# Another leaf order at the end of ff1's last outer product, and a searched order on the engines, in a fp32 transformer block on one core

## The chip, the core and the metric

The kernel runs on one core of one Trainium2 chip. A core has a matrix engine (TensorE, PE in the profile; PEld is its loading of weights), a vector engine (VectorE, DVE), an activation engine (ScalarE, ACT), a general engine (GpSimd, POOL) and a queue engine (SyncE, SP) that here issues nearly all transfers between the chip's main memory and the on-chip memory. Matrix results land in eight accumulation banks (bank0 to bank7), from which VectorE or ACT must read them ("evict" below) before the bank is used for something else.

The metric is the device time of one execution in microseconds (us), the median of several. All numbers below are us unless marked ns.

## The reference

Everything is fp32. `x` is 2 x 2048 x 512, `t` (the input `cond_1024`) 2 x 512, ssm weights 512 x 512, ff weights 512 x 1024 and 1024 x 512.

```python
emb = jnp.dot(jax.nn.silu(t), ada_w) + ada_b
shift_msa, scale_msa, gate_msa, shift_mlp, scale_mlp, gate_mlp = jnp.split(emb, 6, axis=-1)
norm = _ln(x) * (1.0 + scale_msa[:, None]) + shift_msa[:, None]
h = jax.nn.gelu(jnp.dot(norm, ssm_w1) + ssm_b1, approximate=False)
ssm_out = jnp.dot(h, ssm_w2) + ssm_b2
x = x + gate_msa[:, None] * ssm_out
norm2 = _ln(x) * (1.0 + scale_mlp[:, None]) + shift_mlp[:, None]
hf = jax.nn.gelu(jnp.dot(norm2, ff_w1) + ff_b1, approximate=True)
ff_out = jnp.dot(hf, ff_w2) + ff_b2
x = x + gate_mlp[:, None] * ff_out
```

## The kernel before

**Tiles and stages.** The 4096 rows are cut into eight blocks of 512. Per block there are the first normalisation (`norm1`), the two ssm products (`ssm1`, `ssm2`), the second normalisation (`norm2`); then, in four stages of two blocks each, the first feed-forward product (`ff1`) and, block by block, the second (`ff2`). Between these the weights are prepared: `weight2` scales the second ssm weight by the gate, `weight_fw1` and `weight_fw2` do the like for the feed-forward weights and write parts of them to main memory, from where `ff1` loads them again.

**Products of quarters.** Each matrix product is done by a fast scheme with seven products of quarter matrices instead of eight: `first` (L420) and `second` (L430) make the sums of quarters that go in, named P1 to P7 together with the quarters used as they are, and the seven products are added into each other's results. ff1 uses the scheme on two levels: seven outer products, in the order P1, P2, P6, P7, P4, P5, P3 (`OUTER`), each with seven inner ones, the leaves. A leaf is two 128x128x256 matmuls, and a matmul shows as two records in the trace. The inner order is `CARRIED` (L445): P1, P5, P6, P2, P7, P3, P4.

**Banks in a leaf order.** Of one outer product the leaves P1, P6, P7 and P4 add into one bank (called y), P2 into a second (x), which begins as a copy of P1 that ACT makes, and P5 and P3 into a third (v) (`BANK`). After each leaf but P1, VectorE adds the bank to the hidden quarters in `hidden` that this leaf belongs to. So P6 may only start when ACT has copied P1 away, P7 when P6 is evicted, P4 when P7 is evicted, P3 when P5 is. In `ff1` (function `leaf`, L1055) consecutive outer products overlap: the last three leaves of one alternate with the first three of the next. The last outer product has nothing behind it, so its last four leaves stand alone, one right behind the other; the outer product before it (P5) is evicted in pieces of 128x1024.

**Who sets the order.** Nothing is issued where the code calls it. Each helper (`tt` for adds of two tensors at L256, `act` L274, `copy` L283, `mm` L294, `turn_by_pe` L304, `dma` L316) records an operation with a cost in ns per engine it may run on ("v" VectorE, "g" POOL, "a" ACT, "p" TensorE, "s" SP). `tt` on data in on-chip memory may go to VectorE or to POOL. `Plan.order` gives each operation a latest start, from due times on TensorE, and `Plan.simulate` then runs through all operations by these costs and lays down engine and place of each; TensorE's operations keep the order of the code. The resulting order is a fixed program. Transfers are modelled as one pipe of 370 bytes per ns with a flight and a landing time, and eight lanes.

**The start.** L1366 copies a mask; then VectorE makes statistics of four row groups of the first block (`BATCH_NORM_STATS2` L522 and its aggregate L523), POOL and VectorE turn them into scales (L555, L556 on POOL, L558 to L561 on VectorE), VectorE (L581) and ACT (L274) normalise, PE turns the rows (L304), and after the modulation rows of `ada_w` the first ssm product begins. L1354 copies conditions and biases, transposed by PE after a row of warming matmuls, out of a bank into `cols`.

Of the kernel before, what the change touches and what calls it, by code (L numbers as in the profile page):

```python
# [1 line left out]

# [12 lines left out]


class Op:
    __slots__ = ("n", "engs", "fn", "cost", "lat", "shared", "size", "lead", "care", "after", "done", "sooner", "deps", "succ", "late", "on", "start", "end", "note")


class Plan:
# [5 lines left out]


    HOP = 70.0
    ISSUE, FLIGHT, LANDING, RATE, BACKLOG = 640.0, 1300.0, 700.0, 370.0, 4000.0  # L30
    NEAR, SPARE = 30000.0, 1500.0
    RATED, LANDED = 0.5, 4000.0
    LITTLE = 1 << 15
    LANES = 8
    AHEAD, SLACK = 2500.0, 150.0

    def __init__(self, nc):
        self.nc = nc
# [47 lines left out]
        return op  # L86

    def order(self):
        ops = self.ops
        for op in ops:  # L90
            if op.engs == "p":
                op.deps = {d for d in op.deps if ops[d].engs != "p"}
            for d in op.deps:
                ops[d].succ.append(op.n)
        t, due = 0.0, {}
        for op in ops:
            if op.engs == "p":
                due[op.n] = t
                t += op.cost["p"]
        for _ in range(2):  # L100
            for op in reversed(ops):
                late = due.get(op.n, 1e9)
                for s in op.succ:
                    late = min(late, ops[s].late - (1 + op.care) * (self.HOP + min(op.lat.values()) + op.size / self.RATE))
                op.late = late - op.sooner
            self.simulate()
            wait = ops[self.anchor].start - due[self.anchor]
            due = {n: t + wait for n, t in due.items()}
        return sorted(ops, key=lambda op: (op.start, op.n))

    def simulate(self):
        ops, hop = self.ops, self.HOP
        left, ready = [len(op.deps) for op in ops], [0.0] * len(ops)
        free = dict.fromkeys("pvags", 0.0)
        self.lock, pipe, holder = 0.0, 0.0, None
        tensor = [op for op in ops if op.engs == "p"]
        at, pools, found = 0, {e: [] for e in "vags"}, {}
        lanes = [0.0] * self.LANES

        def enter(op):  # L120
            if op.lead and op.late < 1e8:
                ready[op.n] = max(ready[op.n], op.late - op.lead)
            for e in op.engs:
                if e != "p":
                    pools[e].append(op)
                    found.pop(e, None)

        def choose(e):
            pool = pools[e]
            if not pool:  # L130
                return None
            at = {}
# [19 lines left out]
        count = len(ops)  # L152
        while count:
# [12 lines left out]
            if op.size > self.LITTLE:  # L166
                pipe = max(start + self.FLIGHT, pipe) + op.size / self.RATE * (1 + self.RATED * op.care)
                op.end = pipe + self.LANDING + self.LANDED * op.care
                found.pop("a", None), found.pop("s", None)
            else:  # L170
                op.end = start + op.lat[e]
                if op.size and e == "s":
                    op.end = max(op.end, pipe + self.LANDING)
            if op.size:
                lanes = lanes[1:] + [op.end]
                found.pop("a", None), found.pop("s", None)
            if e in op.shared:
# [10 lines left out]
            count -= 1  # L188
# [10 lines left out]
def kernel(  # L199
# [153 lines left out]
    for n in range(8):  # L353
        t = psum.tile([P, 2 * HT], F32, tag=f"bank{n}", name=f"bank{n}")
# [88 lines left out]
            tt(e, o[:, r], a[:, r], b[:, r], f)  # L443

    CARRIED = ("P1", "P5", "P6", "P2", "P7", "P3", "P4")  # L445

# [343 lines left out]

    def ssm1(i, ops, wops, hooks={}, order=CARRIED):
        plan.stage = f"ssm1 {i}"
# [97 lines left out]
    OUTER = ("P1", "P2", "P6", "P7", "P4", "P5", "P3")  # L892
# [131 lines left out]
    def ff1(s):  # L1024
        plan.stage = f"ff1 {s}"
        ops = tokens(s)
# [26 lines left out]
        QUAD = {"P2": "11", "P5": "22", "P6": "12", "P7": "22", "P3": "12", "P4": "21"}  # L1053

        def leaf(n, j):  # L1055
            p, f = OUTER[n], CARRIED[j]
            bank = {"y": Y_AT[n], "x": X_AT[n % 2], "v": V_AT[n % 2]}
            t = pair(bank[BANK[f]])
            src = cut(inner[n][f], "p a (c q) -> p c a q", q=G)
            half, at = divmod(FW1_AT[f], 4)  # L1060
            for h in range(2):
                mm(t[:, h, :], slot[n][half][:, at, h * P : (h + 1) * P], src, f in ("P1", "P5") and h == 0, f in ("P2", "P3", "P4"))
            if f == "P1":
                copy(pair(bank["x"]), t)
# [352 lines left out]
    for i in range(1, NBLK):  # L1417
# [4 lines left out]
        last = i + 2 >= NBLK  # L1422
# [76 lines left out]
```

## Time and profile before

| | |
|---|---|
| median of 3 executions | 566.46 (566.42 to 566.55) |
| profiled execution, own time | 566.59 |
| its span, first to last instruction | 564.8 |
| PE busy | 557.8, 99% |
| DVE busy | 483.1, 86% |
| POOL busy | 379.0, 67% |
| ACT busy | 266.0, 47% |
| granted TensorE clock | 1.000 |
| moved by transfers | 119.85 MB, mean 212 GB/s |

The profiled execution is 0.13 above the median, and 1.8 of it lie outside the span. A row of the timeline reads: start from the span's beginning, length, engine, line, operation, output tile, input tiles, shapes, and how many equal neighbours it joins; in brackets the idle time of the engine before it and what ended that. Matmuls are pipelined and their ends are modelled, so a row of PE is read by its start against the start of the next.

### The profile page before, as it was taken

What the parts mean: (1) busy time and instruction counts of PE and PEld (TensorE: products, weight loads), DVE (VectorE), ACT (ScalarE), POOL (GpSimd) and SP (SyncE); (2) the same over time, 40 slices, a digit from 0 to 9 for tenths busy, and PEclk for the clock granted to TensorE, in tenths of its full rate; (3) what the DMA queues carried; (4) which work ended last, traced back from release to release, by engine and by line L of the source; (5) the groups of instructions that cost most, each with busy time, mean ns of one, the idle gap of its engine ahead of it and who ended that gap; (6) DMA issues with size and microseconds to landing.
All of it is one profiled execution on the core that took longest, in us unless ns stands there. A gap on an engine that the chain in (4) does not pass through costs nothing.

```text
span 564.8 us, 10322 instructions
## 1 busy us (share of the span) xinstructions
PE 557.8 (99%) x3553; PEld 506.3 (90%) x3553; DVE 483.1 (86%) x918; ACT 266.0 (47%) x534; POOL 379.0 (67%) x514
## 2 busy tenths in 40 slices
PE   8999999999999999999999999999999999999997
PEld 4888889888898988889999889999889999888997
DVE  5696978888879989898989899999999888789776
ACT  3473856674888845557102347212366122336120
POOL 2887638979826687995547866776776784446660
PEclk9999999999999999999999999999999999999999
DMA  8953799989799879895047899078956041820022
GB/s 315 398 221 87 233 343 308 316 240 320 223 268 369 257 271 273 273 323 185 4 147 255 302 286 332 18 204 282 321 172 198 2 151 46 272 95 28 1 75 74
DMA packets 53057, 119.85 MB, mean 212 GB/s; under 512 B 5473, under 2 KB 10509, under 8 KB 51470
## 3 DMA queue, kind: packets, MB, share of 16 engines
q1 hardware_dynamic: 51842, 118.66, 63.9%
q8 instruction: 28, 0.46, 0.3%
q10 hardware_dynamic: 1164, 0.55, 0.3%
q14 instruction: 23, 0.19, 0.1%
HBM read 77.63 MB, written 40.51 MB: 209 GB/s over the span
## 4 chain that ended last, share of the span: by engine, by line
PE 94%; DVE 3%; DMA 1%; issue 1%; POOL 0%; SPq 0%; DVEq 0%
PE bank L294 94%; DMA fw<-in_L_cond_ada_w_dram 1%; DVE hidden L256 1%; DVE near L256 0%; DVE marks L522 0%; PE bank L304 0%; POOL hidden L256 0%; POOL near L256 0%; SPq L316 0%; DVE rows L256 0%; DVE ring L256 0%; DVE fw L256 0%; DVE far L591 0%; DVE turned L656 0%; DVE marks L523 0%
## 5 line engine op out<-in xcount | busy, mean ns | idle before, releaser
L294 PE MATMUL bank<-turned,ring 128*128 128x256 f32 x896 | 208.7, 380 | 0.2 <-DVE turned L656 0.2
L294 PEld LDWEIGHTS bank<-turned,ring 128*128 128x128 f32 x896 | 167.6, 190 | 22.9 <-DVE turned L656 0.5
L256 DVE TENSOR_TENSOR hidden<-bank,hidden 128x512 f32<-128x512 f32 (+1 forms) x171 | 125.2, 755 | 28.0 <-PE bank L294 24.8
L294 PE MATMUL bank<-near,hidden 128*128 128x256 f32 (+1 forms) x470 | 95.3, 350 | 0.3 <-DVE rows L256 0.2
L294 PEld LDWEIGHTS bank<-near,hidden 128*128 128x128 f32 x470 | 82.1, 190 | 10.0 <-DVE rows L256 0.6
L294 PE MATMUL bank<-fw,hidden 128*128 128x128 f32 x640 | 90.4, 275 | 0.0
L256 DVE TENSOR_TENSOR rows<-bank,rows 128x128 f32<-128x128 f32 (+3 forms) x154 | 78.8, 554 | 11.4 <-PE bank L294 10.9
L294 PE MATMUL bank<-ring 128*128 128x256 f32 x336 | 82.4, 381 | 0.5 <-DVE hidden L256 0.5
L294 PEld LDWEIGHTS bank<-fw,hidden 128*128 128x128 f32 x640 | 81.2, 192 | 0.4
L283 ACT COPY bank<-bank 128x512 f32<-128x512 f32 (+2 forms) x88 | 37.3, 425 | 83.3 <-PE bank L294 82.2
L256 POOL TENSOR_TENSOR turned<-turned 128x512 f32<-128x512 f32 (+1 forms) x56 | 63.1, 1139 | 16.7 <-ACT turned L274 9.4
L294 PEld LDWEIGHTS bank<-ring 128*128 128x128 f32 x336 | 63.2, 190 | 11.2 <-issue 1.7
L294 PE MATMUL bank<-fw,far 128*128 128x128 f32 (+2 forms) x644 | 67.6, 278 | 0.7 <-DMA fw<-in_L_cond_ada_w_dram 0.7
L294 PEld LDWEIGHTS bank<-fw,far 128*128 128x128 f32 (+1 forms) x644 | 60.9, 167 | 2.7 <-issue 1.7
L274 ACT ACTIVATE hidden<-hidden,cols 128x512 f32<-128x512 f32 (+1 forms) x66 | 45.0, 712 | 37.9 <-DVE hidden L256 37.8
L294 PE MATMUL bank<-fw,near 128*128 128x128 f32 (+1 forms) x452 | 61.1, 279 | 0.0
L256 POOL TENSOR_TENSOR hidden<-hidden 128x128 f32<-128x128 f32 (+2 forms) x52 | 43.6, 847 | 22.6 <-DVE hidden L256 6.4
L294 PEld LDWEIGHTS bank<-fw,near 128*128 128x128 f32 x452 | 56.0, 192 | 0.4
L256 POOL TENSOR_TENSOR fw<-fw 128x256 f32<-128x256 f32 (+1 forms) x52 | 45.0, 875 | 13.3 <-DVE fw L256 7.7
L274 ACT ACTIVATE turned<-turned,mod,mod 128x512 f32<-128x512 f32 x56 | 41.5, 805 | 8.2 <-DMA turned<-turned 7.2
L256 POOL TENSOR_TENSOR ring<-turned,ring 128x256 f32<-128x256 f32 x37 | 27.8, 757 | 15.8 <-PE bank L294 9.7
L256 DVE TENSOR_TENSOR hidden<-hidden 128x512 f32<-128x512 f32 (+2 forms) x58 | 34.9, 621 | 1.2 <-ACT hidden L274 0.8
(136 smaller groups left out, 692.4 us busy)
## 6 DMA issues: line engine op xcount, KB each, us to landing
ring<-fw_parts SPq DMA_DIRECT2D x28, 512.0 KB
turned<-far SPq DMA_DIRECT2D x52, 256.0 KB
ring<-fw_parts SPq DMA_DIRECT2D x28, 384.0 KB
rows<-x SPq DMA_DIRECT2D x32, 256.0 KB
turned<-turned SPq DMA_DIRECT2D x32, 256.0 KB
out_dram<-rows SPq DMA_DIRECT2D x28, 256.0 KB
fw_parts<-fw SPq DMA_DIRECT2D x21, 256.0 KB
fw<-in_L_cond_ada_w_dram SPq DMA_DIRECT2D x5, 1024.0 KB
```

The lines of the kernel that those rows point to most:

```text
L256: lambda E: E.tensor_tensor(o, a, b, f),
L274: lambda E: E.activation(o, a, func, bias=bias, scale=scale),
L283: plan.add("a", lambda E: E.copy(o, a), [o], [a], {"a": cost}, {"a": cost + 60})
L294: lambda E: E.matmul(o, lhsT, rhs, start=start, stop=stop, skip_group_check=True, **kw),
```

## The change

1. The leaves of ff1's last outer product take the order `ALONE`: P1, P6, P5, P7, P2, P3, P4. So P6 changes places with P5, and P7 with P2. The other outer products keep `CARRIED`.
2. The planner no longer makes one plan. It makes a first one, measures it in `follow` under four assumptions (`CASES`: landing time, transfer rate, length of the work on VectorE, ACT and POOL), notes the gaps on TensorE that are over 30 ns, and then 600 times asks some operations in front of a gap to come sooner (or their rivals later), draws up the plan again, and keeps it if TensorE ends earlier, at first also if it ends slightly later. The best is issued.
3. `WAKE`: the modelled transfer pipe delivers nothing before 2.2 us.

Only places and engines of operations differ: 109 adds go from POOL to VectorE and 85 from VectorE to POOL. TensorE has the same matmuls, in the same order but for 1.

```diff
+    WAKE = 2200.0
+    ROUNDS, WARMTH, LEAST = 600, 300.0, 30.0
+    CASES = ((700.0, 1.0, 1.0), (2200.0, 1.0, 1.0), (1200.0, 0.85, 1.0), (700.0, 1.0, 1.03))
...
+        self.draw_up({})
+        wait = ops[self.anchor].start - ops[self.anchor].due
+        for op in tensor:
+            op.due += wait
+        draw = random.Random(1)
+        wanted, (cost, gaps) = {}, self.draw_up({})
+        best = cost, wanted
+        for n in range(self.ROUNDS):
+            other = dict(wanted)
...
+                other[sooner] = other.get(sooner, 0.0) + more
+            found = self.draw_up(other)
+            if found[0] <= cost + draw.random() * self.WARMTH * (1 - n / self.ROUNDS):
+                wanted, (cost, gaps) = other, found
+                if cost < best[0]:
+                    best = cost, wanted
+        self.draw_up(best[1])
         return sorted(ops, key=lambda op: (op.start, op.n))
+
+    def draw_up(self, wanted):
+
+        ops = self.ops
+        for op in reversed(ops):
+            late = min([ops[s].late for s in op.succ], default=1e9) - op.ahead
+            op.late = (op.due if op.engs == "p" and op.due < late else late) - op.sooner - wanted.get(op.n, 0.0)
+        self.simulate()
+        last = dict.fromkeys("pvags")
+        for op in self.sequence:
+            op.before, last[op.on] = last[op.on], op.n
+        cost, gaps = 0.0, []
+        for case in self.CASES:
+            cost += self.follow(*case, gaps) / len(self.CASES)
+        return cost, gaps
...
-        self.lock, pipe, holder = 0.0, 0.0, None
+        self.lock, pipe, holder = 0.0, self.WAKE, None
...
     CARRIED = ("P1", "P5", "P6", "P2", "P7", "P3", "P4")
+    ALONE = ("P1", "P6", "P5", "P7", "P2", "P3", "P4")
...
         def leaf(n, j):
-            p, f = OUTER[n], CARRIED[j]
+            p, f = OUTER[n], (CARRIED, ALONE)[n == 6][j]
```

More of the change, by code (lines that the diff above doesn't have):

```diff
@@ L1 @@
+import random
 from contextlib import ExitStack
@@ L17 @@
 class Op:
-    __slots__ = ("n", "engs", "fn", "cost", "lat", "shared", "size", "lead", "care", "after", "done", "sooner", "deps", "succ", "late", "on", "start", "end", "note")
+    __slots__ = ("n", "engs", "fn", "cost", "lat", "shared", "size", "lead", "care", "after", "done", "sooner", "deps", "succ", "ahead", "before", "due", "late", "on", "start", "end", "note")
 class Plan:
     HOP = 70.0
+    WAKE = 2200.0
     ISSUE, FLIGHT, LANDING, RATE, BACKLOG = 640.0, 1300.0, 700.0, 370.0, 4000.0
@@ L94, in order @@
                 ops[d].succ.append(op.n)
-        t, due = 0.0, {}
+        tensor = [op for op in ops if op.engs == "p"]
+        t = 0.0
+        for op in tensor:
+            op.due, t = t, t + op.cost["p"]
         for op in ops:
[L97 to L108, printed above, removed]
@@ L109, in order @@
-        return sorted(ops, key=lambda op: (op.start, op.n))
+            op.ahead = (1 + op.care) * (self.HOP + min(op.lat.values()) + op.size / self.RATE)
+        self.draw_up({})
+        wait = ops[self.anchor].start - ops[self.anchor].due
+        for op in tensor:
+            op.due += wait
[4 more added lines that the diff above has]
+            other = dict(wanted)
+            if other and draw.random() < 0.3:
+                del other[draw.choice(list(other))]
+            for d, over in draw.choices(gaps, [g[0] for g in gaps])[0][1]:
+                more = over * draw.choice((0.5, 1.0, 1.5, 3.0))
+                for _ in range(draw.choice((1, 1, 2, 3, 4, 6, 9))):
+                    sooner, rival = d, ops[d].before
+                    held = [u for u in ops[d].deps if ops[u].engs != "p"]
+                    last = max(held, key=lambda u: ops[u].end, default=None)
+                    if rival is not None and (last is None or ops[rival].start + ops[rival].cost[ops[rival].on] > ops[last].end):
+                        if draw.random() < 0.5:
+                            sooner, more = rival, -more
+                            break
+                        last = rival
+                    if last is None:
+                        break
+                    d = last
+                other[sooner] = other.get(sooner, 0.0) + more
[4 more added lines that the diff above has]
+                    best = cost, wanted
@@ new lines, in follow @@
+    def follow(self, landing, pace, longer, gaps):
+        ops, hop, end = self.ops, self.HOP, [0.0] * len(self.ops)
+        free = dict.fromkeys("pvags", 0.0)
+        pipe, lock, lanes = self.WAKE, 0.0, [0.0] * self.LANES
+        for op in self.sequence:
+            e, ready = op.on, 0.0
+            last = longer * op.cost[e] if e in "vag" and not op.size else op.cost[e]
+            for d in op.deps:
+                t = end[d] if ops[d].on == e and not ops[d].size else end[d] + hop
+                if t > ready:
+                    ready = t
+            start = max(free[e], ready)
+            if op.size:
+                start = max(start, lanes[0])
+                pipe = max(start + self.FLIGHT, pipe) + op.size / (self.RATE * pace)
+                end[op.n] = (pipe if op.size > self.LITTLE else start + op.lat[e]) + landing
+                lanes = lanes[1:] + [end[op.n]]
+            else:
+                if e in op.shared:
+                    start = max(start, lock)
+                    lock = start + last
+                end[op.n] = start + last + op.lat[e] - op.cost[e]
+            if e == "p" and start > free[e] + self.LEAST and op.n > self.anchor:
+                gaps.append((start - free[e], [(d, end[d] + hop - free[e]) for d in op.deps if end[d] + hop > free[e]]))
+            free[e] = start + last
+        return free["p"]
@@ L151, in simulate @@
                 enter(op)
-        count = len(ops)
-        while count:
+        self.sequence = []
+        while len(self.sequence) < len(ops):
             best = None
@@ L187, in simulate @@
                     found.pop(x, None)
-            count -= 1
+            self.sequence.append(op)
             for s in op.succ:
```

## The prediction

> **What bounds the kernel now.** First the page's busy times and the chain that ended last:
>
> ```profile
> PE 557.8 (99%) x3553; PEld 506.3 (90%) x3553; DVE 483.1 (86%) x918; ACT 266.0 (47%) x534; POOL 379.0 (67%) x514
> PE 94%; DVE 3%; DMA 1%; issue 1%; POOL 0%; SPq 0%; DVEq 0%
> ```
>
> TensorE is both the busiest engine and 94% of the chain, so only its gaps can be won or lost. The change neither adds nor removes a matmul. Busy time hides gaps, so I took the timeline of PE and looked for rows that begin later than their predecessor allows. Each matmul shows as two records.
>
> ```profile
> 28.58 3.62 PE L294 MATMUL bank<-near,hidden 128*128 128x256 f32 x16
> 32.04 1.04 PE L304 MATMUL bank<-far 128*128 128x128 f32 x8
> 33.12 3.72 PE L294 MATMUL bank<-near,hidden 128*128 128x256 f32 x16
> ...
> 31.77 2.53 POOL L256 TENSOR_TENSOR near<-near 128x512 f32<-128x512 f32 x2
> ...
> 36.84 0.87 PE bank L304 x8
> ```
>
> Sixteen 256-column records take 32.04 - 28.58 = 3.46, so one takes 0.216 us. Eight transposes take 0.87 where nothing waits (last line, from the chain in order of time), so PE could have gone on at 32.91; it did at 33.12: 0.21 lost, and 0.10 more on the restart (3.72 against 3.62 for the same sixteen). It waited for the first of POOL's two adds, which ends at about 33.07. Gap one: 0.31.
>
> ```profile
> 204.75 3.19 PE L294 MATMUL bank<-near,hidden 128*128 128x256 f32 x14
> 208.17 1.13 PE L294 MATMUL bank<-near,hidden 128*128 128x256 f32 x4 [0.24 <-DVE rows L256]
> ...
> 206.86 0.68 DVE L591 STREAM_TRANSPOSE far<-near 128x512 f32<-128x512 f32 x1
> 207.46 0.65 DVE L256 TENSOR_TENSOR rows<-bank,rows 128x512 f32<-128x512 f32 x1
> ```
>
> 204.75 + 14 x 0.216 = 207.77 against 208.17: 0.40, with a restart 0.50. An eviction stood behind a transpose on VectorE. Then the end of ff1, in all four stages:
>
> ```profile
> 252.37 2.75 PE L294 MATMUL bank<-turned,ring 128*128 128x256 f32 x12
> 255.36 1.10 PE L294 MATMUL bank<-ring 128*128 128x256 f32 x4 [0.24 <-DVE hidden L256]
> ...
> 339.68 2.75 PE L294 MATMUL bank<-turned,ring 128*128 128x256 f32 x12
> 342.68 0.89 PE L294 MATMUL bank<-ring 128*128 128x256 f32 x3 [0.24 <-DVE hidden L256]
> ...
> 426.56 2.77 PE L294 MATMUL bank<-turned,ring 128*128 128x256 f32 x12
> 429.34 0.89 PE L294 MATMUL bank<-ring 128*128 128x256 f32 x3
> ...
> 513.13 2.77 PE L294 MATMUL bank<-turned,ring 128*128 128x256 f32 x12
> 515.91 0.89 PE L294 MATMUL bank<-ring 128*128 128x256 f32 x3
> ...
> 250.84 4.37 DVE L256 TENSOR_TENSOR hidden<-bank,hidden 128x1024 f32<-128x1024 f32 x5 [0.50 <-PE bank L294]
> ```
>
> The twelve records are the leaves P2, P7, P3 of the last outer product, the next row is P4, which adds into the bank that P7's eviction must have read. Twelve records end 2.59 after their start, so P4 is late by 0.40, 0.41, 0.19 and 0.19: 1.19. The chain of five VectorE evictions ends at 255.21, just before P4.
>
> **The change, part by part.**
>
> (1) P7 ahead of P2. Between P7 and P4 there are then two leaves (1.73 us) where there was one (0.86). In stages 2 and 3 VectorE is hardly late, so one leaf more covers it. In stages 0 and 1 the chain of five (two of about 1.2, three of about 0.6 from start to start) loses a member: in the new order P6's small eviction stands ahead of it, and in stage 0 P7's also goes ahead of the last long one. It ends by 254.6, before P4's 254.96. The 1.19 goes, with four restarts of 0.07 (the row at 255.36 has 1.10 for four records; the clean row quoted below at (4) has 1.89 for eight, less 4 x 0.216 = 1.03). Gain 1.47. Next after P4 comes ff2's first product, whose operands are long ready.
>
> (2) The order from 600 plans. 109 adds go from POOL to VectorE and 85 back: 24 more on VectorE. In the new order weight2's second sum, which PE waits for at 33.12, is on VectorE right behind its four scalings, over a microsecond earlier; the next add there has 0.8 to spare. Gain 0.31. At 207.46 the transpose no longer stands ahead of the eviction; it comes about 0.6 earlier, enough for 0.50. Gains so far: 1.47 + 0.31 + 0.50 = 2.28.
>
> (3) The later first loads. SP's first 50 issues keep their order, and no load starts later on the chip: the planner only believes that x lands 2.2 us later, and orders VectorE by that. The copy of the columns (L1354) moves from behind two more statistics to the place right behind the first.
>
> ```profile
> 5.51 0.66 DVE L522 BATCH_NORM_STATS2 marks<-far 128x6 f32<-128x512 f32 x1
> 6.95 0.30 DVE L523 BATCH_NORM_AGGREGATE marks<-marks 128x2 f32<-128x6 f32 x2
> 7.57 0.20 DVE L1354 COPY cols<-bank 128x44 f32<-128x44 f32 x1 [0.32 <-PE bank L304]
> 7.68 0.68 DVE L522 BATCH_NORM_STATS2 marks<-far 128x6 f32<-128x512 f32 x1
> 8.62 0.15 DVE L558 TENSOR_TENSOR marks<-marks 128x2 f32<-128x2 f32 x1
> 9.40 0.55 DVE L581 TENSOR_SCALAR far<-far,marks 128x512 f32<-128x512 f32 x1
> ...
> 7.20 0.19 POOL L555 TENSOR_SCALAR marks<-marks 128x2 f32<-128x2 f32 x1 [5.39 <-DVE marks L523]
> 7.47 0.73 POOL L556 TENSOR_TENSOR marks<-marks,small 128x2 f32<-128x2 f32 x1
> ...
> 9.51 0.80 ACT L274 ACTIVATE far<-far,marks 128x512 f32<-128x512 f32 x1
> ...
> 11.17 1.09 PE L304 MATMUL bank<-far 128*128 128x128 f32 x8
> ```
>
> That copy waits for PE until 7.57 whatever stands behind it, so the statistics that ran at 5.51 now start at 7.68, the third row's at 8.3, the aggregate at 8.9 instead of 6.95. POOL follows by the distances of these rows: L555 at 9.15, L556 at 9.42, ending 10.15. VectorE's L558 comes at 10.2 (was 8.62), and ACT's normalisation, 0.78 behind it, at 11.0, ending 11.8. PE's second transpose needs that and ran at about 11.3; the later steps of the start move along. Cost 0.50. It is at least 0.3 and at most 0.8 (no idle time or all of ACT's 0.80 uncovered); a gain is excluded, since nothing on this chain starts earlier.
>
> (4) P6 directly behind P1 in the last outer product. P6 adds into the bank that ACT's copy of P1 must have read, with one leaf between instead of more. The first outer product of each stage has the same distance already:
>
> ```profile
> 247.19 1.89 PE L294 MATMUL bank<-turned,ring 128*128 128x256 f32 x8
> ...
> 214.32 1.95 PE L294 MATMUL bank<-ring 128*128 128x256 f32 x8
> ...
> 474.97 2.06 PE L294 MATMUL bank<-ring 128*128 128x256 f32 x8
> ```
>
> Eight clean records take 1.89; with that wait 1.95 to 2.06: 0.06 to 0.17 each. I take 0.06, as the new instruction waits for the same two engines as the row at 214.32: 4 x 0.06 = 0.24, at most 0.68.
>
> (5) The end of ff2 at 385.6.
>
> ```profile
> 384.26 1.06 PE L294 MATMUL bank<-fw,hidden 128*128 128x128 f32 x8
> 385.60 1.27 PE L294 MATMUL bank<-fw,hidden 128*128 128x128 f32 x8
> ```
>
> Here 0.21 is lost already, to an eviction. The new order puts two more adds of weights ahead of it than it takes away work: about 0.2 more; 0 to 0.4.
>
> (6) Two covers that become thin. SP: the third load of ff_w1 now stands ahead of block 3's token load and two stores behind it; elsewhere SP exchanges stores, gate rows and x loads between 60 and 240 us, with room; ACT's issues keep their order and POOL has none. The stores that this load waits for follow transposes that the order places about 1.0 later.
>
> ```profile
> 70.64 0.44 SPq L316 DMA_DIRECT2D turned<-turned  x1
> ...
> 79.62 2.93 ACT L274 ACTIVATE turned<-turned,mod,mod 128x512 f32<-128x512 f32 x4 [5.26 <-DMA turned<-turned]
> ...
> 81.95 2.54 PE L294 MATMUL bank<-turned,ring 128*128 128x256 f32 x11
> ```
>
> ACT's second piece ends near 81.1 and PE needs it at 82.4: about 1.2 of cover for about 1.0 to 1.3 of delay. And VectorE:
>
> ```profile
> 171.24 1.72 DVE L256 TENSOR_TENSOR turned<-turned 128x512 f32<-128x512 f32 x1
> ...
> 174.09 0.69 DVE L256 TENSOR_TENSOR far<-bank,far 128x512 f32<-128x512 f32 x1 [0.52 <-PE bank L294]
> ```
>
> The first of these two and a weight add now stand directly ahead of the eviction, which PE needs one product (1.73) after its data: 0.84 of cover for about 0.86. Together 0.25, between 0 and 1.0.
>
> (7) What the order hides. The present order left two stalls that are no one's structure, 0.50 and 0.21; the new one is as dense, so I add their like, less what (5) and (6) hold: 0.45, between 0 and 1.2.
>
> Sum: 0.50 + 0.24 + 0.20 + 0.25 + 0.45 = 1.64 lost, 2.28 won: 0.64 less. The profiled execution took 566.59 and would take 565.95; the median is 0.13 lower (0.02%), so 565.8.
>
> **The rivals.**
>
> *Start and order cost little.* If ACT's end at 11.8 is partly covered and (7) is empty, 0.3 + 0.24 + 0.20 + 0.10 are lost: 565.0. For it: the planner charged stalls in its search. Against: the copy's wait at 7.57 is in the trace.
>
> *VectorE and POOL block each other: slower.* The 128x512 add at 171.24 took 1.72 where an eviction of that size takes 0.65 (207.46): more than a microsecond for one meeting with POOL. With 24 more adds on VectorE, each such hit on an eviction that PE waits for costs 0.3 to 0.5 after its cover. It decides from 2.2 us of them, five to seven hits: 2.5 gives 566.46 - 2.28 + 1.19 + 2.5 = 567.9. Against: POOL has 24 adds fewer, so meetings need not be more, and most evictions have over 0.5 of cover. The Trainium skill, "SBUF — State Buffer", section "Who interferes with whom", says that a VectorE instruction with two SBUF inputs and a GpSimd one that reads SBUF exclude each other for a whole instruction; by that rule every such pair costs up to a whole add. The row of 1.72 agrees with it.
>
> *It does nothing.* P4's wait is exchanged for copies of 0.17 each (0.68), and the gaps at 33 and 208 reappear a few microseconds off (0.81): -2.28 + 0.68 + 0.81 + 0.50 + 0.20 = -0.09: 566.4.
>
> **How the numbers follow.** 0.2% is 1.13 us: faster means below 565.33, slower above 567.59; a measurement of this kernel tells about that from no change. The sum has a chance of 0.62, with 565.0 to 566.6 as its own range (terms 1 to 4 nearly fixed, 5 to 7 free), of which 0.10 lies below 565.33. The cheap start has 0.16, the port 0.14, no effect 0.08. Faster: 0.10 + 0.16 = 0.26, same 0.52 + 0.08 = 0.60, slower 0.14. The range 564.8 to 567.0 leaves out a twentieth below and most of the port rival.
>
> **What would show it.** In the new trace P4 follows twelve records after 2.59 in all four stages, with a row of 1.95 or more where P6 starts; PE's first long products start near 14.6 instead of 14.07; the rows near 33 and 208 have no gap. The forecast is wrong if PE starts at 14.07, if rows with an idle time before them turn up elsewhere, or if adds of 1.2 us and more stand ahead of evictions that PE waits for.

## The result and the profile after

The changed kernel takes 568.02 us (median of 7 runs, 567.82 to 568.50), the kernel before beside it 566.46 (566.42 to 566.64). The ratio is 1.0028, with an interval of 1.0019 to 1.0037: slower by 1.56 us, 0.28%, and so beyond the bound of 0.2% (567.59). I had predicted 565.8, with a range of 564.8 to 567.0: the time moved the other way. The profiled executions took 567.98 and 566.59, a difference of 1.39, of which 1.09 lie in the span (565.86 against 564.77) and 0.30 outside it.

First the page of the changed kernel, busy times and chain:

```profile
PE 557.2 (98%) x3553; PEld 506.2 (89%) x3553; DVE 491.0 (87%) x942; ACT 263.9 (47%) x534; POOL 363.3 (64%) x490
PE 93%; DVE 3%; POOL 2%; DMA 1%; ACT 0%; issue 0%; ACTq 0%; DVEq 0%; POOLq 0%
```

TensorE still bounds the kernel; its share of the chain fell by a hundredth, and POOL now has a part in the chain. Which waits those are, the view of PE's waits tells (total us, times, longest). Lines of the code now stand 72 or 73 further down: L366 is the matmul, L376 the transpose, L328 the add.

```profile
PE bank L366 <- DVE rows L328: 1.4, 1, 1.4
...
PE bank L376 <- DMA fw<-in_L_cond_ssm_b_dram: 0.7, 1, 0.7
PE bank L376 <- DVE far L654: 0.7, 1, 0.7
```

The first is new and single: one wait of 1.4 us for an eviction. The timeline around it, in the changed kernel:

```profile
383.93 5.14 POOL L328 TENSOR_TENSOR fw<-fw 128x256 f32<-128x256 f32 x6
...
384.44 0.94 DVE L328 TENSOR_TENSOR fw<-fw 128x256 f32<-128x256 f32 x1
385.31 0.94 DVE L328 TENSOR_TENSOR turned<-turned 128x256 f32<-128x256 f32 x1
385.74 0.61 PE L366 MATMUL bank<-fw,hidden 128*128 128x128 f32 x4
386.17 0.94 DVE L328 TENSOR_TENSOR fw<-fw 128x256 f32<-128x256 f32 x1
387.04 3.40 DVE L328 TENSOR_TENSOR rows<-bank,rows 128x256 f32<-128x256 f32 x6
387.70 0.71 PE L366 MATMUL bank<-fw,hidden 128*128 128x128 f32 x4 [1.35 <-DVE rows L328]
```

and at the same place in the kernel before:

```profile
384.82 0.41 DVE L256 TENSOR_TENSOR ring<-turned,ring 128x256 f32<-128x256 f32 x1
385.16 0.41 DVE L256 TENSOR_TENSOR turned<-turned 128x256 f32<-128x256 f32 x1
385.50 5.66 DVE L256 TENSOR_TENSOR rows<-bank,rows 128x256 f32<-128x256 f32 x10
...
385.65 2.50 POOL L256 TENSOR_TENSOR turned<-turned 128x512 f32<-128x512 f32 x2 [1.90 <-DVE turned L256]
```

Before, two 256-wide adds of VectorE stand ahead of the evictions, 0.34 from start to start, and POOL begins when they are over. Now there are three, 0.87 from start to start, and POOL's six sums run through all of them. The evictions come at 387.04, and PE stands from 386.19 (four records after 385.74) to 387.70: 1.51, with its restart of 0.10 1.62, where 0.21 were lost before.

The start, in the timeline of the changed kernel:

```profile
7.58 0.23 PE L376 MATMUL bank<-far,fw 44*128 44x44 f32 x1 [0.69 <-DMA fw<-in_L_cond_ssm_b_dram]
...
7.85 0.20 DVE L1427 COPY cols<-bank 128x44 f32<-128x44 f32 x1 [2.12 <-PE bank L376]
7.97 1.28 DVE L595 BATCH_NORM_STATS2 marks<-far 128x6 f32<-128x512 f32 x2
...
9.42 0.19 POOL L628 TENSOR_SCALAR marks<-marks 128x2 f32<-128x2 f32 x1 [7.62 <-DVE marks L596]
...
11.24 0.81 ACT L346 ACTIVATE far<-far,marks 128x512 f32<-128x512 f32 x1 [1.35 <-DVE marks L634]
...
14.89 0.92 PE L366 MATMUL bank<-turned,ring 128*128 128x256 f32 x3 [0.21 <-DVE turned L729]
```

VectorE stands idle for 2.12 us in front of the copy, and the first long product is 0.82 later than before (14.07). The copy itself is 0.28 later than before (7.57), because PE's transposition had to wait for the last part of the small bias load until 7.58.

The end of ff1, PE alone, in the first stage:

```profile
249.03 1.10 PE L366 MATMUL bank<-ring 128*128 128x256 f32 x4
...
252.56 2.75 PE L366 MATMUL bank<-turned,ring 128*128 128x256 f32 x12
255.15 1.03 PE L366 MATMUL bank<-ring 128*128 128x256 f32 x4
```

P4 follows the twelve records after 2.59, with no idle time and no restart, and so it does in the other three stages. P6 at 249.03 has 1.10 for four records, a restart of 0.07, and begins 0.05 late; the same stands at 336.44, 424.70 and 511.01. Last, two places where PE now waits for POOL; the first of them:

```profile
254.28 1.28 POOL L328 TENSOR_TENSOR near<-hidden,near 128x512 f32<-128x512 f32 x1
...
255.37 0.75 DVE L328 TENSOR_TENSOR hidden<-hidden 128x512 f32<-128x512 f32 x1
...
256.26 1.26 POOL L328 TENSOR_TENSOR near<-near 128x512 f32<-128x512 f32 x1 [0.69 <-DVE hidden L328]
256.46 1.83 PE L366 MATMUL bank<-fw,near 128*128 128x128 f32 x12
```

POOL ends a sum at 255.56 and starts the next, which needs that one, at 256.26: the order holds it behind the add of VectorE at 255.37. The sum ends at 257.52. Twelve clean records take 1.50; here they show 1.83, which is an idle time of 0.22 at 257.58 and a restart of 0.10. At 345.88 PE waits for POOL again, 0.23 and a restart, but for another reason:

```profile
344.82 1.55 DVE L328 TENSOR_TENSOR near<-near 128x256 f32<-128x256 f32 x2
344.87 0.96 POOL L328 TENSOR_TENSOR near<-hidden 128x256 f32<-128x256 f32 x1
```

POOL's 256-wide sum takes 0.96 beside two adds of VectorE. Where only evictions run beside them, six such sums take 4.28 (the run with POOL held, below), 0.71 each.

The account of the span, by starts of PE's records: start +0.82, the wait at 387.70 +1.41, the two waits for POOL +0.65, four waits of P6 for the copy of P1 +0.50 (0.125 each), a restart at 299.65 +0.10; P4 -1.45, the two gaps at 33 and 208 -0.81, two small ones at 432 and 518 -0.12. Sum +1.10 for 1.09 measured.

### The profile page after: what moved, and what is told of

Read it like the earlier page. It is cut to its first block, busy times and chain, and to the rows that moved or that the text cites. A ratio compares the mean times of both kernels' runs of the same rounds, so it can differ in the third digit from the quotient of the medians.

```text
span 565.9 us, 10332 instructions
## 1 busy us (share of the span) xinstructions
PE 557.2 (98%) x3553; PEld 506.2 (89%) x3553; DVE 491.0 (87%) x942; ACT 263.9 (47%) x534; POOL 363.3 (64%) x490
## 4 chain that ended last, share of the span: by engine, by line
PE 93%; DVE 3%; POOL 2%; DMA 1%; ACT 0%; issue 0%; ACTq 0%; DVEq 0%; POOLq 0%
PE bank L366 92%; POOL near L328 1%; DMA fw<-in_L_cond_ssm_b_dram 1%; PE bank L376 1%; DVE turned L328 1%; DVE hidden L328 0%; DVE rows L328 0%; DVE fw L328 0%; ACT hidden L346 0%; POOL hidden L328 0%; ACTq L388 0%; DVE marks L595 0%; DVE ring L328 0%; DVE bank L328 0%; POOL marks L629 0%
## 5 line engine op out<-in xcount | busy, mean ns | idle before, releaser
L366 PE MATMUL bank<-turned,ring 128*128 128x256 f32 x896 | 208.6, 380 | 0.2 <-DVE turned L729 0.2
L366 PEld LDWEIGHTS bank<-turned,ring 128*128 128x128 f32 x896 | 167.7, 190 | 22.8 <-DVE turned L729 0.4
L328 DVE TENSOR_TENSOR hidden<-bank,hidden 128x512 f32<-128x512 f32 (+1 forms) x171 | 123.9, 754 | 23.5 <-PE bank L366 20.6
L366 PE MATMUL bank<-near,hidden 128*128 128x256 f32 (+1 forms) x470 | 95.0, 349 | 0.0
L366 PE MATMUL bank<-fw,hidden 128*128 128x128 f32 x640 | 90.5, 275 | 1.4 <-DVE rows L328 1.4
L366 PEld LDWEIGHTS bank<-near,hidden 128*128 128x128 f32 x470 | 82.2, 190 | 9.2
L328 DVE TENSOR_TENSOR rows<-bank,rows 128x128 f32<-128x128 f32 (+3 forms) x154 | 78.7, 555 | 10.0 <-PE bank L366 8.7
L366 PEld LDWEIGHTS bank<-fw,hidden 128*128 128x128 f32 x640 | 81.3, 192 | 1.9 <-DVE rows L328 1.5
L366 PE MATMUL bank<-ring 128*128 128x256 f32 x336 | 82.4, 381 | 0.0
L366 PEld LDWEIGHTS bank<-ring 128*128 128x128 f32 x336 | 63.1, 190 | 10.4 <-POOL near L328 0.8
L366 PE MATMUL bank<-fw,far 128*128 128x128 f32 (+2 forms) x644 | 67.6, 278 | 0.3 <-DMA fw<-in_L_cond_ada_w_dram 0.3
L328 POOL TENSOR_TENSOR turned<-turned 128x512 f32<-128x512 f32 (+1 forms) x52 | 58.5, 1137 | 9.4 <-ACT turned L346 4.1
L366 PEld LDWEIGHTS bank<-fw,far 128*128 128x128 f32 (+1 forms) x644 | 60.9, 167 | 2.3 <-issue 1.1
L366 PE MATMUL bank<-fw,near 128*128 128x128 f32 (+1 forms) x452 | 61.5, 279 | 0.1
L328 POOL TENSOR_TENSOR hidden<-hidden 128x512 f32<-128x512 f32 (+2 forms) x51 | 45.5, 900 | 23.4 <-DVE hidden L328 9.2
L366 PEld LDWEIGHTS bank<-fw,near 128*128 128x128 f32 x452 | 56.1, 192 | 0.9 <-POOL near L328 0.5
L328 POOL TENSOR_TENSOR fw<-fw 128x256 f32<-128x256 f32 (+1 forms) x41 | 36.3, 897 | 11.2 <-DVE fw L328 6.9
L328 POOL TENSOR_TENSOR ring<-turned,ring 128x256 f32<-128x256 f32 x37 | 27.0, 739 | 22.1 <-PE bank L366 15.0
L346 ACT ACTIVATE hidden<-bank,cols 128x256 f32<-128x256 f32 x62 | 26.1, 471 | 19.2 <-PE bank L366 19.2
```

The source lines that it names most:

```text
L328: lambda E: E.tensor_tensor(o, a, b, f),
L346: lambda E: E.activation(o, a, func, bias=bias, scale=scale),
L366: lambda E: E.matmul(o, lhsT, rhs, start=start, stop=stop, skip_group_check=True, **kw),
```

## The experiments

The runs with the changed kernel write down the order that the 600 rounds found, so it is the same order, and alter it at its end, in `order`, as the diffs say. `ops[n]` is an operation by its number in the program, `start` its place in the order, `on` its engine, and `after` an additional wait of POOL for VectorE.

**The start put back.**

```diff
         self.draw_up(best[1])
+        for n, late in ((28, 0.02), (92, 0.04), (29, 0.06), (93, 0.08)):  # statistics, aggregates
+            ops[n].start = ops[38].start - 0.1 + late                      # 38: copy of cols
```

> The changed kernel with one thing put back: VectorE copies the columns out of the bank behind the statistics of the second and third row and two aggregates, as before, instead of right behind the first aggregate. Nothing else moves. Theory (the place of the copy costs the start): PE's first long product goes back from 14.89 to 14.07 (within 0.1), the time falls by 0.8 to 567.2, and the repeats lie closer together than the 0.7 us of the changed kernel, because the landing of the small bias load is no longer in front of the statistics. Rival (the start is late because PE's transposition of the rows came at 7.58 instead of 7.30, the bias load having landed late): the first long product stays at 14.6 or later, the time within 0.3 of 568.0.

Measured: 567.15 (567.09 to 567.77, 11 runs), 0.87 less than the changed kernel. The timeline of this run:

```profile
8.21 0.20 DVE L1427 COPY cols<-bank 128x44 f32<-128x44 f32 x1 [0.96 <-PE bank L376]
...
14.07 1.13 PE L366 MATMUL bank<-turned,ring 128*128 128x256 f32 x4 [0.21 <-DVE turned L729]
```

Here PE's transposition came later still, the copy at 8.21, and the first product is at 14.07 all the same. So the rival is out: the late load costs only because the statistics stand behind the copy. Of eleven repeats nine lie within 0.2 us; the changed kernel's seven spread over 0.7.

**POOL held behind the evictions.**

```diff
         self.draw_up(best[1])
+        ops[2900].after = ops[2859]  # first of POOL's six sums; second eviction
```

> The changed kernel with one wait more: POOL's first sum of ff_w2's parts (383.93 in the changed kernel) waits for VectorE's second eviction of the bank (the one at 387.37). VectorE's order stays, with the two additional adds ahead of the evictions. Theory (POOL's six sums and VectorE's three adds shut each other out): VectorE's three 256-wide adds take 0.41 to 0.45 instead of 0.94, the eviction comes at about 385.9 instead of 387.04, PE's idle time at 387.70 falls from 1.35 to 0.2 or less, and the time falls by 1.2 to 1.5, to about 566.7. POOL's sums come about 2 us later, and nothing waits for them. Rival one (two more adds in VectorE's queue cost it, whatever POOL does): the adds stay at 0.9 and the idle time above 1.0, the time within 0.3 of 568.0. Rival two (PE is only late by something else a moment later): the idle time goes, but a new one of about 1 us turns up within the next 10 us.

Measured: 566.44 (566.04 to 567.07, 11 runs), 1.58 less than the changed kernel. Its timeline (L327 and L365 are the add and the matmul here):

```profile
385.11 0.41 DVE L327 TENSOR_TENSOR fw<-fw 128x256 f32<-128x256 f32 x1
385.45 0.41 DVE L327 TENSOR_TENSOR turned<-turned 128x256 f32<-128x256 f32 x1
385.78 0.41 DVE L327 TENSOR_TENSOR fw<-fw 128x256 f32<-128x256 f32 x1
...
386.12 5.66 DVE L327 TENSOR_TENSOR rows<-bank,rows 128x256 f32<-128x256 f32 x10
386.42 1.08 PE L365 MATMUL bank<-fw,hidden 128*128 128x128 f32 x8
386.81 4.28 POOL L327 TENSOR_TENSOR fw<-fw 128x256 f32<-128x256 f32 x6 [2.17 <-DVE rows L327]
```

The same three adds in the same queue take 0.41, the idle time of PE is gone, and POOL's sums, 2.2 later against PE, delay nobody. Neither the length of VectorE's queue nor the transfers that run there made the stall: both are unchanged. The evictions, which read one input from a bank, take the same time beside POOL's sums as without them. The Trainium skill says of this in "SBUF — State Buffer", section "Who interferes with whom", that a VectorE instruction with two SBUF inputs contends with a GpSimd one that reads SBUF, and that one with at most one SBUF input doesn't, outside the modes that use two ports; the trace agrees.

**POOL held for one add only.**

```diff
+        ops[2900].after = ops[2908]  # the first of VectorE's three adds
```

> The changed kernel with POOL's first sum of ff_w2's parts held only behind the first of VectorE's three 256-wide adds (384.44 in the changed kernel), not behind the evictions: two of the three adds can still meet POOL's sums instead of three. Theory (every add that meets POOL's sums back to back costs about 0.53): the first add takes 0.41, the second and third 0.8 to 0.95, the eviction comes 0.5 earlier, PE's idle time at 387.70 is 0.8 to 0.9, the time 0.5 less: 567.5. Rival (the first meeting alone costs, or the meetings share one cost): either nothing is won (568.0), or nearly all of the 1.58 (566.6).

Measured: 567.07 (566.64 to 568.20, 11 runs), 0.95 less than the changed kernel.

```profile
384.95 0.41 DVE L327 TENSOR_TENSOR turned<-turned 128x256 f32<-128x256 f32 x1
385.11 2.39 POOL L327 TENSOR_TENSOR fw<-fw 128x256 f32<-128x256 f32 x3 [0.96 <-DVE fw L327]
385.29 0.94 DVE L327 TENSOR_TENSOR fw<-fw 128x256 f32<-128x256 f32 x1
...
386.82 0.71 PE L365 MATMUL bank<-fw,hidden 128*128 128x128 f32 x4 [0.26 <-DVE rows L327]
```

I had counted two meetings; there was one, since the second add had begun when POOL was let go. So three meetings cost PE 1.62, one 0.52, none nothing: about 0.54 for each, as the theory has it, though the run is not the one I had expected.

**Both corrections.** The two diffs together.

> The changed kernel with both corrections at once: the copy of the columns behind the statistics as before, and POOL's first sum of ff_w2's parts behind VectorE's eviction. Theory (the two costs are independent): 0.87 and 1.58 less than the changed kernel's 568.02: 565.6, and the repeats within 0.5 us. Rival (what is won at the start is lost at the next wait for a transfer, since the transfers do not come earlier): only one of the two gains, 566.4 or more.

Measured: 565.55 (565.50 to 566.02, 11 runs); the two gains add up to 565.57. The ratio to the kernel before is 0.9982 (0.9973 to 0.9990).

**The order of the leaves alone, and the new order with the old leaves.** Two first builds of these left the evictions in their places while the products changed theirs, so that some evictions read a bank after the next leaf had added into it: these two compute part of ff1 wrongly, and their times (570.85 and 569.33) say nothing on the leaves.

> The kernel before with the order of the leaves alone changed in the last outer product (P1, P6, P5, P7, P2, P3, P4): each leaf takes the place, on PE and on VectorE, of the leaf that stood there, and every other instruction keeps its engine and its place. Theory: P4's four idle times and their restarts go (1.45), four waits of 0.126 of P6 for the copy of P1 come (0.50): 0.95 less, 565.5. My prediction's sizes give 1.47 - 0.24 = 1.23 less: 565.2. Rival (the waits are only exchanged): within 0.3 of 566.46.

> The changed kernel with the old order of leaves put back in the last outer product, each leaf in the place of the one that stands there; the order on the engines is the new one. Theory (the two parts add up): the four idle times of P4 are back, 0.95 more than the changed kernel: 569.0, which is 2.5 above the kernel before; the order alone then costs +2.5. Rival (the new order on the engines covers the old order of leaves as well): within 0.3 of 568.0.

The second builds move the evictions of P6 and P7 with their products:

```diff
-    for op in plan.order():
+    planned = plan.order()
+    for s in range(0, 28, 7):
+        groups = [plan.ops[n : n + 3] for n in last_leaves[s : s + 7]]  # a leaf: 2 products, 1 eviction
+        work = [[op.fn for op in group] for group in groups]
+        begin = [group[0].start for group in groups]
+        read = [group[2].start for group in groups]
+        for group, name in zip(groups, wanted):  # wanted: the other order
+            n = names.index(name)
+            for op, fn in zip(group, work[n]):
+                op.fn = fn
+            moved = group[0].start - begin[n] if name in ("P6", "P7") else 0.0
+            group[2].start = max(read[n] + moved, group[1].start + 0.01)
+    planned.sort(key=lambda op: (op.start, op.n))
+    for op in planned:
```

> The kernel before with the order of the leaves alone changed in the last outer product (P1, P6, P5, P7, P2, P3, P4) on PE; the evictions of P6 and P7 move forward on VectorE by as much as their products do, the other evictions and every other instruction keep engine and place. Theory: P4's four idle times and their restarts go (1.45), four waits of 0.126 of P6 for the copy of P1 come (0.50): 0.95 less than the kernel before, 565.6. My prediction's sizes give 1.47 - 0.24 = 1.23 less: 565.3. Rival (the idle times are only exchanged for others at the same place): within 0.3 of the kernel before.

> The changed kernel with the old order of leaves put back on PE in the last outer product; the evictions of P6 and P7 move back on VectorE by as much as their products do, everything else stays, so the order on the engines is the new one. Theory (the two parts add up): P4's idle times are back and the waits for the copy go, about 0.95 more than the changed kernel: 569.0. Rival (the new order on the engines covers the old leaves too): within 0.3 of 568.0.

Measured: the leaves alone 565.89 (ratio to the kernel before 0.9989, 0.9978 to 0.9999), 0.6 less; the new order with the old leaves 570.83, 2.8 more than the changed kernel and 4.3 more than the kernel before. PE's row of P4 in the second stage, the leaves alone first, then the old leaves in the new order:

```profile
342.40 1.10 PE L294 MATMUL bank<-ring 128*128 128x256 f32 x4
```

```profile
343.62 1.10 PE L364 MATMUL bank<-ring 128*128 128x256 f32 x4 [0.84 <-DVE hidden L326]
```

With the leaves alone three of P4's four idle times go; the second stage keeps 0.06 and a restart, a wait of PE for POOL at 344.77 takes 0.19, and four waits of P6 cost 0.50: -1.45 + 0.50 + 0.14 + 0.19 = -0.62. In the new order the old leaves wait 0.40, 1.00, 1.01 and 1.01: the order was drawn up for the new leaves and puts their evictions later. So the two parts don't add up in these builds, against my theory, and a cost of "the order alone" can't be told from these runs.

**Four corrections.** Both, and the two waits for POOL:

```diff
+        ops[1967].on, ops[1967].start = "v", ops[1941].start - 1.0  # the sum PE waits for at 257.58
+        ops[1967].after = ops[2549].after = None
+        ops[1956].start = ops[1941].start + 1.0                      # the add that kept POOL waiting
+        ops[1968].after = ops[1961]
+        ops[2549].on, ops[2549].start = "v", ops[2558].start - 1.0   # the sum PE waits for at 345.88
```

> As the run with both corrections, and two more at the places where PE waits for POOL's sums (257.58 and 345.88 in the changed kernel): at the first the sum that PE waits for goes from POOL to VectorE, ahead of an eviction, and the add that kept POOL waiting goes behind that eviction, with POOL's next sum held until VectorE's following add; at the second the sum that PE waits for goes from POOL to VectorE. Theory: both idle times with their restarts go (0.33 each), 0.65 less than the run with both corrections: about 564.9, 0.3% under the kernel before. Rival (VectorE's evictions behind the sums come too late in their turn): no gain, within 0.2 of the run with both.

Measured: 565.02 (median of 12 runs, all but one within 564.88 to 565.33), ratio to the kernel before 0.9973 (0.9964 to 0.9983): this version is faster than the kernel before and than the changed kernel. Where the twelve records had shown 1.83, this run's timeline has

```profile
258.41 1.50 PE L372 MATMUL bank<-fw,near 128*128 128x128 f32 x12
```

(its profiled execution is the odd one of the twelve, with the first long product only at 16.83; the last section comes back to it). Both waits are gone, 0.65; but at 279.05 and 301.50 evictions are now late by 0.21 and 0.14, which with restarts is 0.55 where there was 0.10. So the span falls from 563.4 to 563.2 only, against the theory; the other 0.3 of the 0.53 lie outside the span, of which the last section speaks.

**Six corrections, and a wait that got lost.**

```diff
+        ops[2109].start = ops[2078].start + 1.0  # an add behind ff2's evictions at 279
+        ops[2288].start = ops[2234].start + 1.0  # another at 301
+        for op in ops:
+            if op.after and op.after.start >= op.start:
+                op.after = None
```

> As the run with four corrections, and two more: where evictions of ff2 came late at 279.05 and 301.50 in that run's profile, the 512-wide add of VectorE that stands directly ahead of them goes behind them; the adds have over 3 us until their results are read. Theory: the idle times of 0.21 and 0.14 with their restarts go (0.45), 564.55. Rival (the lateness is earlier in VectorE's queue and only moves): within 0.2 of 565.02.

Measured: 570.81, 5.8 more than with four: neither theory. POOL's sum 2290 had an additional wait for the add 2288, which now came later in the order, so the wait fell. POOL's sum 2124 lost its wait for the other moved add, 2109, in the same way: that add took 1.51 beside POOL, at 276.18, and while the idle time at 279 went (0.31 with its restart), two waits of PE, for copies that ACT made late behind VectorE's evictions, came at 279.34 and 280.80, 1.06 with their restarts. No run separates wait and move there. For the larger stall, near 303, two runs separate the wait from the move of 2288:

```diff
+        ops[2290].start = ops[2288].start + 1.0  # four corrections, and 2288 late,
+        ops[2290].after = ops[2288]              # POOL still waits for it
```

> As the run with four corrections, and one more: at 301.50 VectorE's 512-wide add that stands ahead of ff2's evictions goes behind the first two of them, and POOL's next sum still waits for that add. Theory (the wait for VectorE decides): no stall of microseconds at 303; the idle time of 0.14 and its restart go: 0.24 less than the run with four, 564.8. Rival (the place of the add made the stall of 3.7): it is there again, 568.5.

```diff
+        ops[2290].after = None                   # the changed kernel without this wait
```

> The changed kernel with one wait less: POOL's first 512-wide sum of rows near 298.9 no longer waits for VectorE's add before it; it needs nothing that this add writes. Order and engines stay. Theory (POOL's adds shut VectorE's adds out unless the order holds them back): POOL's 512-wide adds start some 2 us earlier, VectorE's three 256-wide adds ahead of ff2's evictions take 1.2 to 1.6 each instead of 0.41, PE stalls for 3 to 3.7 near 302, and the time is about 571.3. Rival (the stall in the run with six came from the moved add): within 0.3 of 568.0.

Measured: 565.50 with the wait kept, 0.5 more than with four, and 574.14 without it, 6.1 more than the changed kernel. The timeline without the wait:

```profile
296.28 4.53 POOL L327 TENSOR_TENSOR rows<-rows,near 128x512 f32<-128x512 f32 x3
296.79 1.48 DVE L327 TENSOR_TENSOR ring<-turned,ring 128x256 f32<-128x256 f32 x1
...
298.20 4.82 DVE L327 TENSOR_TENSOR turned<-turned 128x256 f32<-128x256 f32 x3
...
304.21 1.01 PE L365 MATMUL bank<-fw,hidden 128*128 128x128 f32 x3 [4.14 <-DVE rows L327]
```

and with four corrections, the add late and the wait kept:

```profile
296.04 1.61 DVE L337 TENSOR_TENSOR turned<-turned 128x256 f32<-128x256 f32 x3
...
298.89 3.74 POOL L337 TENSOR_TENSOR rows<-rows,near 128x512 f32<-128x512 f32 x3 [3.65 <-DVE rows L337]
```

Three adds (one of 256 columns and two of 512, not three of 256 as I had put it) took 4.82 beside POOL's 512-wide sums and 1.61 with POOL held: the wait decides, and the moved add 2288 is cleared of the large stall. It won nothing all the same: the idle time at 301 went, but POOL's sums came later, ACT's work later too (I read this from their starts and did not test it), and PE waited for the copy of P1 at 319.49 and 320.69, 0.73 together.

**The copy of P1 in halves**, on top of the six corrections:

```diff
-                copy(pair(bank["x"]), t)
+                copy_by_halves(pair(bank["x"]), t)  # one copy of 256 columns for each product of P1
```

> As the run with six corrections, and ACT's copy of P1 at ff1 is made in two halves, one for each product of P1, each with its own wait, instead of one copy of 512 columns behind both. Theory (P6 directly behind P1 waits for the end of ACT's whole copy, 0.05 and a restart of 0.075 at each end of ff1 and about 0.1 at each first outer product): the first half is ready before P6's first product, and 0.5 to 0.9 go: about 563.9. Rival (ACT's additional instruction costs as much, 0.2 of fixed time each, or the wait is one of both halves): within 0.2 of the run with six.

Measured: 572.33, 1.5 more than with six. ACT's copy of P1 in the first stage in the changed kernel, then ACT and PE in halves:

```profile
248.32 0.57 ACT L355 COPY bank<-bank 128x512 f32<-128x512 f32 x1
```

```profile
247.63 0.75 ACT L370 COPY bank<-bank 128x256 f32<-128x256 f32 x2
...
248.52 1.10 PE L381 MATMUL bank<-ring 128*128 128x256 f32 x4
```

The halves take 0.75 for 0.57, and P6 starts 0.14 behind the end of the second one, as it had started 0.14 behind the whole copy (248.89, 249.03). The first half began no sooner behind P1 than the whole copy: from the start of the copying to P6 it is 0.89 here and 0.71 in the changed kernel, and the difference is the 0.18 that the halves take longer. The rival was right: the wait of 0.05 became 0.23. Why the first half doesn't start sooner, and why P6's first product waits for the second half, was not tried.

## Why the prediction was wrong

- **Step 5, the end of ff2, failed.** "About 0.2 more; 0 to 0.4" was 1.41 more. I counted two more adds ahead of an eviction and looked at VectorE's queue alone. POOL's sums, which in the kernel before began behind these adds, now ran beside them, and each of three adds cost 0.53 more. The order has no wait between the two there: the planner keeps such adds of the two engines apart in its plan, but it writes a wait into the program only where POOL was held back for that in the plan. Here it was not: the planner lets POOL's first sum begin when it believes that a load of ff_w2 has landed, which in its plan is 0.5 after the last of the adds. On the chip POOL came 2.1 earlier against VectorE than planned, and nothing held it. Held, the stall is gone and 1.58 are won.
- **The rival of VectorE and POOL blocking each other** had the mechanism, and 567.9 with a chance of 0.14. Its count was off: I had 2.5 spread over five to seven meetings. Three adds in one place made 1.41 of 2.06, and the two waits for POOL made the other 0.65: there POOL is the one that is held, once by a wait of the order and once by meeting VectorE's adds. That 567.9 lies so near to 568.02 is luck in part, for the later start and the time outside the span fill up what was missing. My argument against it, that POOL has 24 adds fewer, has no force: what decides is not how many adds there are but whether a wait keeps them apart.
- **Step 3, the start**, was right in its mechanism and too small: 0.82 for 0.50, and 0.87 in the run that puts it back. I took the copy's time of 7.57 as given; it hangs on a small load that landed later here, the copy came 0.28 later, and the new order has nothing else to do in that time.
- **Step 1** was right, 1.45 for 1.47, but only together with the new order: alone the leaves took 1.31 of P4's waits away and, with P6's waits and one for POOL, gave 0.6 in all. **Step 4** was right in kind and half the size: 0.125 each and not 0.06, inside its bounds. **Step 2** was right, 0.81 for 0.81.
- **Step 6** did not come: neither place shows a gap. In one execution, that of the profile with POOL held, about 0.6 were lost at 58.8 behind a late transfer of tokens instead. **Step 7**, 0.45 for what can't be seen, was 0.63: 0.65 + 0.10 - 0.12. That it came near is luck: it was sized by two late evictions, and what came were waits for POOL.
- **Outside the span** 0.30 came on top, which no step had.

From 0.64 less to 1.39 more it is 2.03. Step 5 has 1.21 of it, the start 0.32, the time outside the span 0.30, step 4 0.26, step 7 0.18 and step 1 0.02; step 6 gives back 0.25. That makes 2.04.

## What to carry to other kernels

An add on VectorE that reads two operands from SBUF has two prices, its own and the one beside POOL; before pricing it, look at which wait keeps POOL's neighbour away, and if the only thing that does is a time in a plan, take the higher price. A planned start that rests on a pessimistic landing of a load is no barrier: where two engines must not meet, write the wait. Put an instruction that waits for a small load behind all the work that doesn't need it, for a copy that came 0.36 later still cost nothing here once it stood there.

## What the runs showed of the hardware

The price of a meeting goes with the length of POOL's instruction. Beside POOL's 256-wide sums a 256-wide add of VectorE came every 0.87 (0.34 alone), 0.53 for each meeting. Beside 512-wide ones the next add began 1.41 after the 256-wide one at 296.79, and the three adds that followed took 4.82 for 1.61: 1.07 for each meeting, whatever the width of VectorE's add. VectorE gets one instruction in between two of POOL's. That agrees with the page of the Trainium skill named above, by which the one that has the ports holds them for its whole instruction.

A stall of PE that is long enough costs twice. After the idle time of 4.14 without the wait, and after 3.53 with six corrections, the view by windows shows (PE, PEld, DVE, ACT and POOL busy, then the granted clock, DMA share and GB/s):

```profile
304.50:310.00 5.50, 5.50 (x20) 4.87 (x20) 4.93 (x8) 0.57 (x1) 0.00 (x0) 0.50 0.13 50
```

```profile
304.50:310.00 5.50, 5.50 (x31) 4.66 (x30) 5.50 (x11) 2.58 (x5) 1.97 (x2) 1.00 0.18 67
```

In the first the clock is halved for some 6 us and 20 records run in place of 31; in the second it is not, but the other four executions of that kernel had mean clocks of 0.994 to 0.997 and took 0.8 to 1.9 us longer than this one (569.96). Two more executions show that the length of one stall doesn't decide alone. The first line is the same stretch with the copy of P1 in halves, where PE had also stood idle for 3.53; the second is from the start of the profiled execution with four corrections, where PE had stood idle for 1.92, until 10.52:

```profile
304.50:310.00 5.50, 5.49 (x24) 4.62 (x24) 4.87 (x9) 1.79 (x4) 1.59 (x2) 0.78 0.25 88
...
12.00:14.00 2.00, 2.00 (x22) 1.61 (x15) 0.96 (x5) 0.81 (x1) 0.00 (x0) 0.50 1.05 391
```

The Trainium skill, "TensorE: Matmul & The Clock Gate", Part 1, gives an idle window of about 3.4 us that runs free of the program. That 3.53 is followed by the half clock in one execution and not in another agrees with a window that runs free; the half clock after 1.92 doesn't fit one in which PE must stand idle throughout. What counts as idle stays open here.

What lies outside the span comes in two sizes: 1.8 us in the kernel before, with the leaves alone, with four and six corrections, with the late add and with the copy in halves; 2.1 in the changed kernel, with the start put back, POOL held (either way), both, the old leaves, and without the wait. Instruction counts and the bytes of instructions loaded don't tell the two groups apart. So 0.3 of the 1.56 stays unexplained, and so does 0.3 of what the version with four corrections wins on the one with two.
